# Causal attention on one Trainium2 core: scores from 64 contraction rows per head, two heads on the two halves of TensorE's rows

## The chip, the cores and the metric

The kernel runs on one core of one Trainium2 chip. The metric is the device time of one execution in microseconds (us), given as the median of several runs. The engines are PE (TensorE: matrix products and transposes), ACT (ScalarE), DVE (VectorE), POOL (GpSimd) and SP, whose queue issues the DMAs. PEld in the profile is PE's loading of weights. The memories on the core are SBUF (128 partitions), and PSUM, into which PE writes, in banks of 128 x 512 float32.

## The reference, cut to what matters

One block of a Perceiver-like model on 256 tokens of width 512: a cross-attention with sigmoid weights over 25,088 context rows, a causal self-attention with 16 heads, a compressed key/value path and rotary parts, and a mixture of eight experts of which each token takes one. The change lies in the second line.

```python
x = x + xattn(layernorm(x), ctx, ctx, Wq, bq, Wk, bk, Wv, bv)      # over 25,088 context rows
x = x + attn(layernorm(x), W_kv_down, W_k_up, W_v_up, W_q, W_q_rope, W_k_rope, W_o)
x = x + ffn(layernorm(x), gate_w, wg, wu, wd)

def attn(x, ...):                                     # D_C = 128, D_R = 32, NH = 16, HD = 32
    c_kv = x @ W_kv_down
    k_rope = rotary(c_kv @ W_k_rope)                  # one for all heads
    k = (c_kv @ W_k_up).reshape(B, T, NH, HD)
    v = (c_kv @ W_v_up).reshape(B, T, NH, HD)
    q = (x @ W_q).reshape(B, T, NH, HD)
    q_rope = rotary(x @ W_q_rope)                     # one for all heads
    scores = einsum('bqhd,bkhd->bhqk', q, k) + einsum('bqr,bkr->bqk', q_rope, k_rope)[:, None]
    scores = where(causal, -inf, scores / sqrt(HD + D_R))
    w = softmax(scores)
    return einsum('bhqk,bkhd->bqhd', w, v).reshape(B, T, 512) @ W_o
```

A head's scores are a product over 64 numbers: 32 of its own query and key, and the 32 rotary ones that all heads share.

## The kernel before, in words

**Main loop.** The context is taken in 49 chunks of 512 rows. Products of the first stage are made of three float32r matmuls on high and low parts (`mm3`, L98 to L100). The loop ends in a stretch written as named steps, and only this stretch is changed.

**Order table.** All after the loop is cut into steps, functions such as `Sp`, `Sv` or `PTc`. The string `ORDER` lists their calls, `name:arguments`, and this list is the program order; `in_order` pins every engine to it. A last argument `a` or `v` puts a copy on ACT or DVE. The engines run their parts of the list side by side and wait for each other by data. The 256 tokens are two halves, called chains 0 and 1 (argument `tt`).

**Steps of the attention**, for chain `tt`:
- `Vp`, `N1v`, `N1g`, `N1w`, `Xp`, `Xc`: end of the cross-attention, layer norm, transposed activations `xT`.
- `CKp`/`CKc`: `c_kv`. `Kp`/`Kc`: keys of all heads, product and copy into the score operand. `VSp`/`VSc`: values. `Qp`/`Qc`: queries of the 16 heads as four groups `g` of four heads.
- `KRp`, `KRv`, `KRc` and `QRp`, `QRv`, `QRc`: rotary keys and queries: product, rotation on DVE with the table `trig`, copies into the score operands.
- `Sp` (scores and mask), `Sv` (row maximum, DVE), `Sa` (exponentials with sums, ACT), `PTp`/`PTc` (transposed weights), `PVp` (weights times values). Chain 0 has 128 keys and four units `u` of four heads; chain 1 has 256 keys and eight units of two heads.
- `R1v`, `R2p`, `R2c`, `ATv`, `ATa`, `ATw`, `WOp`: normalisation and output product. `N2v` and the rest: layer norm, routing (`LG`, `RK`, `RW`, `RP`), gathering tokens by expert (`GA`), expert products (`GU`, `DN`) and putting back (`SC`, `OU`). `WOs`, `RWs`, `RDs` issue DMAs on SP: output weights, and the weights of experts chosen at run time (`mg`, `mh`, `md`).

**Score operands before.** A query tile `qs` of 128 partitions holds, for two heads at a time, their 64 own rows and the rotary rows, with zeros elsewhere (POOL memset, L359). The key tiles `kbd` hold in a column block per head its own 32 rows, the rotary rows in the other half of the partitions, and zeros (memset, L340). One float32 matmul over 128 rows gives the scores of two heads:

```python
for h in range(h0, h0 + n, 2):
    mm(p3[:, h - h0:h - h0 + 2, :], lhsT=qs[:, tt, h // 2, g, :], rhs=kbd[g // 2][:, g % 2, h:h + 2, :nk], ...)
```

`bank()` takes one of six PSUM banks shared by all steps; `pr` (exponentials) and `pt` (their transposes) each have two buffers.

Of the kernel before, what the change touches and what calls it, by code (L numbers as in the profile page):

```python
# [37 lines left out]
EXa ZSv ZSp O1:0:a AV:0 ZRv O2p:0 AV:1 O2a:0 AV:2 O2v:0 AV:3 Vp:0:0 Vp:0:1 Vp:0:2 Vp:0:3 AV:4 N1v:0 AV:5 AV:6  # L38
AV:7 N1g:0 N1w:0 O1:1:a Xp:0 O2p:1 Xc:0:a O2a:1 CKp:0 O2v:1 Qp:0:0 CKc:0:v Kp:0:0 Kp:0:1 Kc:0:0:3:a Kc:0:0:1:v
Vp:1:0 Kc:0:1:1:a Kc:0:1:3:v Vp:1:1 Vp:1:2 Vp:1:3 VSp:0 WOs N1v:1 Qp:0:1 VSc:0:a Qp:0:2 N1g:1 Qp:0:3 N1w:1 Xp:1  # L40
Qc:0:0:a Qc:0:1:v KRp:0 QRp:0 Xc:1:a KRv:0 QRp:1 KRc:0:1:0:v KRc:0:0:0:a QRv:0 Kc:0:1:2:a CKp:1 Kc:0:0:2:a
KRc:0:0:1:v QRc:0:0:v QRc:0:1:a Qp:1:0 Kc:0:0:0:a QRv:1 CKc:1:a KRc:0:1:1:v Kp:1:0 QRc:1:1:v QRc:1:0:a Kp:1:1
Kc:0:1:0:a Sp:0:1 Sp:0:3 Kc:1:0:3:a Sv:0:1 Sa:0:1 Sp:0:2 Sv:0:3 Kc:1:1:3:v Qp:1:1 Sa:0:3 Kc:1:1:1:v Sv:0:2
Qp:1:2 PTp:0:3 PTp:0:1 Sa:0:2 PTc:0:3:v Qp:1:3 PTc:0:1:v PVp:0:3 Qc:1:0:a Qc:1:1:v PVp:0:1 KRp:1 PTp:0:2 KRv:1
Sp:0:0 PTc:0:2:a KRc:1:1:0:v KRc:1:1:1:v Kc:1:1:2:a VSp:1 KRc:1:0:1:v Kc:1:1:0:a Kc:1:0:1:a Sv:0:0 Sp:1:4
Kc:1:0:0:a VSc:1:a KRc:1:0:0:v Kc:1:0:2:v Sa:0:0 Sp:1:6 Sv:1:4 Sp:1:2 Sv:1:6 Sa:1:4 R1v:0 PTp:0:0 Sp:1:1 Sv:1:2
Sa:1:6 PTc:0:0:v R2p:0 Sv:1:1 PTp:1:6 R2c:0:a Sp:1:7 Sa:1:2 Sp:1:5 Sv:1:7 PTp:1:2 Sv:1:5 Sp:1:3 Sa:1:7 PVp:0:2
Sv:1:3 PVp:0:0 PTc:1:6:a PTp:1:7 ATv:0 PTc:1:2:a PTp:1:4 Sa:1:5 PVp:1:6 PVp:1:2 PTc:1:4:v Sp:1:0 ATa:0 PTc:1:7:v
Sa:1:1 PTp:1:5 ATw:0 PVp:1:4 Sa:1:3 PVp:1:7 Sv:1:0 WOp:0:0 PTc:1:5:v WOp:0:1 PTp:1:3 PTp:1:1 PTc:1:3:a WOp:0:2
Sa:1:0 WOp:0:3 PVp:1:5 R1v:1 PVp:1:3 PTc:1:1:a PTp:1:0 N2v:0 R2p:1 PTc:1:0:a PVp:1:1 R2c:1:a PVp:1:0 ATv:1 N2g:0  # L50
ATa:1 N2w:0 Ya:0 ATw:1 Yp:0 Yv:0 Yc:0:a WOp:1:0 WOp:1:1 WOp:1:2 WOp:1:3 LGp:0 N2v:1 LGv:0 N2g:1 RKp:0 N2w:1
RKv:0 Yp:1 Ya:1 RWv:0 Yc:1:a RPv:0 RWs:0 LGp:1 Yv:1 PMp:0 GAp:0:0 LGv:1 PMc:0:a GAp:0:1 GAc:0:0:v GAp:0:2
GAc:0:1:a RKp:1 GAp:0:3 GAc:0:2:v GUp:0:0:0 RKv:1 GAc:0:3:a GUp:0:0:1 RWv:1 GUp:0:0:2 RPv:1 RWs:1 GUp:0:0:3
GUp:0:1:0 GEa:0:0 GUp:0:1:1 GEv:0:0 GUp:0:1:2 GUp:0:1:3 GAp:1:2 GEa:0:1 RDs:0 GAp:1:3 GEv:0:1 GAc:1:2:a GAp:1:0
GAc:1:3:a GAp:1:1 GAc:1:0:v ITp:0:1 ITp:0:0 PMp:1 GAc:1:1:a ITc:0:1:v ITc:0:0:v GUp:0:2:0 PMc:1:a GUp:0:2:1
GUp:0:2:2 GUp:0:2:3 DNp:0:0 GEa:0:2 GEv:0:2 GUp:1:1:0 DNa:0:0 RDs:1 GUp:1:1:1 GUp:1:1:2 DNv:0:0 GUp:1:1:3
GUp:1:2:0 GEa:1:1 GUp:1:2:1 GEv:1:1 GUp:1:2:2 GUp:1:2:3 GUp:1:0:0 GEa:1:2 GUp:1:0:1 GEv:1:2 GUp:1:0:2 GUp:1:0:3
DNp:0:1 GEa:1:0 GEv:1:0 ITp:0:2 SCp:0:0:0 DNa:0:1 SCp:0:0:1 ITc:0:2:v ITp:1:0 ITp:1:1 ITp:1:2 DNv:0:1 SCp:0:1:0
ITc:1:0:a ITc:1:2:a DNp:0:2 ITc:1:1:a DNp:1:0 DNa:0:2 DNp:1:1 DNv:0:2 DNa:1:0 DNp:1:2 DNv:1:0 DNa:1:1 SCp:0:1:1
DNa:1:2 DNv:1:1 SCp:0:2:0 SCp:0:2:1 SCp:1:0:0 DNv:1:2 SCp:1:0:1 SCp:1:1:0 SCp:1:1:1 OUv:0 SCp:1:2:0 SCp:1:2:1  # L60
OUs:0 OUv:1 OUs:1
# [17 lines left out]
def body(ctx, tc, a, out, nch=NCH):  # L79
# [25 lines left out]
    def bank(name):  # L105
        return psum.tile([P, D], F32, tag="b", name=name, bufs=6)
# [4 lines left out]
    def toks(t):  # L111
        return slice(t * P, (t + 1) * P)
# [225 lines left out]
    kbd = [sb.tile([P, 2, 4, T], F32, tag="rT", name=f"kbd{i}", bufs=2) for i in range(2)]  # L338
    for i in range(2):
        nc.gpsimd.memset(kbd[i], 0.0)  # L340
# [14 lines left out]
    trig = sb.tile([64, T], F32, tag="qp0", name="trig")  # L355
    nc.sync.dma_start(trig, a["trig"])
    vs = [sb.tile([P, D], F32, tag=f"kp{i}", name=f"vs{i}", bufs=2) for i in range(2)]
    qs = sb.tile([P, 2, 2, KD, P], F32, tag="N0", name="qs", bufs=2)
    nc.gpsimd.memset(qs, 0.0)  # L359
# [95 lines left out]
    @step  # L455
    def N1v(tt):
        tt2(x1[tt], ps_["v", tt], x_sb[tt], ALU.add)
        mo[tt] = var(x1[tt], f"b{tt}")
# [22 lines left out]
    def rotated(n, dst, ps, tt):  # L481
        c = sb.tile([32, P], F32, tag="rc", name=f"rc{n}{tt}")
        s = sb.tile([32, P], F32, tag="rsn", name=f"rsn{n}{tt}")
        tt2(c, ps[0:32], trig[0:32, toks(tt)], ALU.mult)
        tt2(s, ps[32:64], trig[32:64, toks(tt)], ALU.mult)
        tt2(dst, c, s, ALU.add)
# [13 lines left out]
    @step  # L500
    def QRp(tt):
        ps_["qr", tt] = bank(f"qr_ps{tt}")[0:64, 0:P]
        prod(ps_["qr", tt], tt, lambda j: pw["wqr"][:, 64 * j:64 * (j + 1)])

    @step
    def QRv(tt):
        qr[tt] = sb.tile([32, P], F32, name=f"qr{tt}")
        rotated("q", qr[tt], ps_["qr", tt], tt)

    @step  # L510
    def QRc(tt, i, eng):
        r = 64 - 64 * i
        scaled(eng, qs[r:r + 32, tt, i], qr[tt][:, None, :].broadcast_to([32, KD, P]), 0.125)
# [11 lines left out]
    @step  # L525
    def KRc(tt, h, i, eng):
        r = 64 - 64 * i
        cp[eng](kbd[h][r:r + 32, :, 2 - r // 32:4 - r // 32, toks(tt)], kr[tt][:, None, None, :].broadcast_to([32, 2, 2, P]))

    @step  # L530
    def Kp(tt, h):
        ps = ps_["k", tt, h] = bank(f"k_ps{tt}{h}")[:, :2 * P].rearrange("p (g t) -> p g t", g=2)
        for g in range(2):
            mm(ps[:, g, :], lhsT=pw["wku"][:, toks(2 * h + g)], rhs=ckv[tt], start=True, stop=True)

    @step
    def Kc(tt, h, j, eng):
        r = slice(32 * j, 32 * j + 32)
        cp[eng](kbd[h][r, :, j, toks(tt)], ps_["k", tt, h][r])
# [16 lines left out]
    @step  # L556
    def Qc(tt, i, eng):
        r = slice(64 * i, 64 * i + 64)
        scaled(eng, qs[r, tt, i], ps_["q", tt][r], 0.125)
# [3 lines left out]
    pr, pt, sc, mx = {}, {}, {}, {}  # L563

    def heads(tt, u):
        return (u, 0, 4) if tt == 0 else (u // 2, 2 * (u % 2), 2)

    @step
    def Sp(tt, u):
        g, h0, n = heads(tt, u)  # L570
        nk = P * (tt + 1)
        p3 = sc[tt, u] = bank(f"s{tt}_{u}").rearrange("p (h k) -> p h k", h=n)
        if tt == 0:
            mm(p3, lhsT=identb, rhs=mask[:, None, :].broadcast_to([P, n, P]), start=True, stop=False)
        for h in range(h0, h0 + n, 2):
            mm(p3[:, h - h0:h - h0 + 2, :], lhsT=qs[:, tt, h // 2, g, :], rhs=kbd[g // 2][:, g % 2, h:h + 2, :nk],  # L576
               start=tt == 1, stop=tt == 0 and h == 2)
        if tt == 1:
            mm(p3[:, :, P:], lhsT=identb, rhs=mask[:, None, :].broadcast_to([P, n, P]), start=False, stop=True)

    @step
    def Sv(tt, u):
        mx[tt, u] = sm.tile([P, 4], F32, tag="mx", name=f"mx{tt}_{u}", bufs=4)
        nc.vector.tensor_reduce(mx[tt, u][:, :heads(tt, u)[2]], sc[tt, u], AX.X, ALU.max, negate=True)

    @step
    def Sa(tt, u):
        g, h0, n = heads(tt, u)
        pr[tt, u] = sb.tile([P, D], F32, tag="wr", name=f"pr{tt}_{u}", bufs=2).rearrange("p (h k) -> p h k", h=n)
        for i in range(n):  # L590
            h = 4 * g + h0 + i
            nc.scalar.activation(pr[tt, u][:, i, :], sc[tt, u][:, i, :], AF.Exp, bias=mx[tt, u][:, i:i + 1],
                                 accum_out=sums[:, tt, h:h + 1])

    @step
    def PTp(tt, u):
        ps = ps_["pt", tt, u] = bank(f"pt{tt}_{u}")
        for i in range(heads(tt, u)[2]):
            for kt in range(tt + 1):
                nc.tensor.transpose(ps[:, toks(i * (tt + 1) + kt)], pr[tt, u][:, i, toks(kt)], ident)  # L600

    @step
    def PTc(tt, u, eng):
        pt[tt, u] = sb.tile([P, D], F32, tag="z", name=f"pt{tt}_{u}", bufs=2)
        cp[eng](pt[tt, u], ps_["pt", tt, u])

    @step
    def PVp(tt, u):
        g, h0, n = heads(tt, u)
        if pv[tt] is None:  # L610
            pv[tt] = psum.tile([P, KD, P], F32, tag=f"acc{tt}", name=f"pv{tt}")
        for kt in range(tt + 1):
            for i in range(n):
                r = slice(32 * (h0 + i), 32 * (h0 + i + 1))
                mm(pv[tt][r, g, :], lhsT=vs[kt][:, g * P + r.start:g * P + r.stop],  # L615
                   rhs=pt[tt, u][:, toks(i * (tt + 1) + kt)], start=kt == 0, stop=kt == tt)
# [41 lines left out]
    @step  # L658
    def N2v(tt):
        x2[tt] = sb.tile([P, D], F32, tag=f"x{tt}", name=f"x2{tt}")  # L660
        tt2(x2[tt], ps_["wo", tt], x1[tt], ALU.add)
        mo[tt] = var(x2[tt], f"c{tt}")
# [279 lines left out]
```

## Time and profile before

| what | value |
|---|---|
| median of 3 runs | 581.35 us (580.42 to 581.46) |
| the profiled execution | 580.47 us, span 578.5 us |
| PE, DVE, ACT busy | 560.4, 447.3, 388.0 us |
| scores, lines L576 (PE), busy in 490 to 545 us | 8.1 us in 16 passes of 512 columns, 4.1 us in 16 of 256 columns |
| masks, L574 and L579 | 1.5 and 2.2 us |
| first score matmul, first output product of chain 1 (`WOp:1`) | 507.5 us, 540.2 us |

The span runs from the first to the last instruction of one profiled execution; the time of the execution is 2.0 us longer. Times of instructions are given from the start of the span. Matmuls overlap, so their busy time is more than the pace at which they follow each other; the chain of waits gives the pace. A float32 matmul appears as two instructions, called passes below.

### The profile page before, as it was taken

How to read it: one execution, taken by the hardware profiler on the slowest of the kernel's cores; microseconds unless marked ns; L12 is line 12 of the kernel's file. 1: busy time of each engine (PE TensorE's matmuls, PEld its weight loads, DVE VectorE, ACT ScalarE, POOL GpSimd, SP SyncE). 2: the span in 40 equal slices, each digit the busy share in tenths (PEclk: the TensorE clock that was granted, in tenths of full speed). 3: DMA queues.
4: the chain of work that ended last, by engine and by line, in shares of the span. 5: the costliest groups of instructions: out<-in, count | busy, mean ns of one | idle time of the engine just before them, and what ended most of it. 6: DMA issues, size and time to landing. Idle time of an engine off the chain costs nothing.

```text
span 578.5 us, 7915 instructions
## 1 busy us (share of the span) xinstructions
PE 560.4 (97%) x3044; PEld 465.3 (80%) x3044; DVE 447.3 (77%) x513; ACT 388.0 (67%) x497; POOL 22.5 (4%) x36
## 2 busy tenths in 40 slices
PE   4999999999999999999999999999999999999697
PEld 3888888888888888888888888888888887876563
DVE  5899888878787878787878787878787865575754
ACT  5877777777777777777777777777777763376332
POOL 5200000000000000000000000000000023000000
PEclk9999999999999999999999999999999999999889
DMA  8897878876575656565657575756465554300081
GB/s 285 347 368 277 288 278 304 304 257 254 183 251 187 255 180 253 187 247 188 248 190 252 181 254 184 256 181 255 180 257 181 213 193 175 146 2 1 5 306 56
DMA packets 22725, 124.49 MB, mean 215 GB/s; under 512 B 3040, under 2 KB 3232, under 8 KB 9376
## 3 DMA queue, kind: packets, MB, share of 16 engines
q1 hardware_dynamic: 22688, 123.99, 59.4%
q8 instruction: 24, 0.39, 0.3%
q14 instruction: 13, 0.11, 0.1%
HBM read 121.36 MB, written 2.62 MB: 214 GB/s over the span
## 4 chain that ended last, share of the span: by engine, by line
PE 94%; DVE 3%; issue 1%; ACT 1%; DMA 1%; POOL 0%; SPq 0%; DVEq 0%; ACTq 0%; POOLq 0%
PE acc L98 15%; PE acc L99 15%; PE acc L100 15%; PE kp_ps L99 8%; PE kp_ps L98 8%; PE kp_ps L100 8%; PE sc L100 4%; PE sc L99 4%; PE sc L98 4%; PE s L576 2%; PE gu L813 2%; PE q_ps L479 1%; PE pt L600 1%; PE dn L842 1%; PE pv L615 1%
## 5 line engine op out<-in xcount | busy, mean ns | idle before, releaser
L95 DVE TENSOR_TENSOR N<-rN,N 128x2048 fp32r<-128x2048 f32 (+1 forms) x53 | 111.8, 2114 | 57.7 <-ACT N L94 57.6
L98 PE MATMUL acc<-N,z 128*128 128x512 f32 x392 | 153.9, 393 | 0.0
L99 PE MATMUL acc<-N,z 128*128 128x512 f32 x392 | 153.7, 392 | 0.0
L100 PE MATMUL acc<-N,z 128*128 128x512 f32 x392 | 152.5, 389 | 0.0
L95 DVE TENSOR_TENSOR T<-rT,T 128x2048 fp32r<-128x2048 f32 (+1 forms) x49 | 110.3, 2253 | 17.2 <-ACT T L94 17.2
L220 ACT ACTIVATE z<-sc 128x512 f32<-128x512 f32 x98 | 58.7, 599 | 78.8 <-PE sc L100 78.6
L94 ACT CAST N<-rN 128x2048 fp32r<-128x2048 f32 (+1 forms) x55 | 94.4, 1725 | 6.1
L94 ACT CAST T<-rT 128x2048 fp32r<-128x2048 f32 (+1 forms) x55 | 94.1, 1717 | 0.1
L100 PEld LDWEIGHTS acc<-N,z 128*128 128x128 f32 x392 | 73.6, 188 | 16.1
L98 PEld LDWEIGHTS acc<-N,z 128*128 128x128 f32 x392 | 74.0, 189 | 12.3
L99 PEld LDWEIGHTS acc<-N,z 128*128 128x128 f32 x392 | 74.0, 189 | 11.6
L98 PE MATMUL kp_ps<-T,wk 128*128 128x512 f32 x196 | 76.9, 392 | 0.0
L100 PE MATMUL kp_ps<-T,wk 128*128 128x512 f32 x196 | 76.7, 391 | 0.0
L99 PE MATMUL kp_ps<-T,wk 128*128 128x512 f32 x192 | 74.7, 389 | 0.0
L222 DVE TENSOR_TENSOR zacc<-zacc,z 128x512 f32<-128x512 f32 x98 | 67.5, 688 | 7.0 <-ACT z L220 1.5
L95 DVE TENSOR_TENSOR z<-z,z 128x512 fp32r<-128x512 f32 x98 | 67.5, 689 | 0.0
L94 ACT CAST z<-z 128x512 fp32r<-128x512 f32 x98 | 61.0, 623 | 3.1
L211 ACT ACTIVATE kp<-kp_ps,bk 128x512 fp32r<-128x512 f32 x49 | 33.9, 691 | 39.9 <-PE kp_ps L100 39.9
L100 PE MATMUL sc<-qp,kp 128*128 128x256 f32 x196 | 55.8, 285 | 0.1
L99 PE MATMUL sc<-qp,kp 128*128 128x256 f32 x196 | 55.4, 283 | 0.0
L98 PE MATMUL sc<-qp,kp 128*128 128x256 f32 x196 | 54.9, 280 | 0.0
L98 PEld LDWEIGHTS kp_ps<-T,wk 128*128 128x128 f32 x196 | 37.1, 189 | 7.8
(209 smaller groups left out, 561.8 us busy)
## 6 DMA issues: line engine op xcount, KB each, us to landing
rN<-in_ctxN SPq DMA_DIRECT2D x49, 1024.0 KB, 4.8
rT<-in_ctxT SPq DMA_DIRECT2D x47, 1024.0 KB, 4.9
gu<-in_gu SPq DMA_DIRECT2D x4, 1024.0 KB, 7.2
sp_wo<-w_wo SPq DMA_DIRECT2D x8, 256.0 KB, 4.0
wo<-sp_wo SPq DMA_DIRECT2D x2, 1024.0 KB, 6.0
mg<-in_gu SPq DMA_DIRECT2D x4, 512.0 KB, 4.0
md<-in_dn SPq DMA_DIRECT2D x6, 256.0 KB, 7.2
rT<-in_ctxT SPq DMA_DIRECT2D x4, 256.0 KB, 6.1
```

The lines of the kernel that those rows point to most:

```text
L94: copy(hi, src)
L95: eng.tensor_tensor(lo, src, f(hi), ALU.subtract)
L98: mm(ps, lhsT=ahi, rhs=bhi, start=first, stop=False)
L99: mm(ps, lhsT=ahi, rhs=blo, start=False, stop=False)
L100: mm(ps, lhsT=alo, rhs=bhi, start=False, stop=last)
L211: nc.scalar.activation(kp[c][0], ps, AF.Identity, bias=bk)
L220: nc.scalar.activation(z, ps, AF.Sigmoid, scale=1.0 / math.sqrt(128.0))
L222: tt2(zacc, zacc, z, ALU.add)
L479: mm(ps, lhsT=w(j), rhs=xT[tt][:, j, :], start=j == 0, stop=j == KD - 1)
L576: mm(p3[:, h - h0:h - h0 + 2, :], lhsT=qs[:, tt, h // 2, g, :], rhs=kbd[g // 2][:, g % 2, h:h + 2, :nk], start=tt == 1, stop=tt == 0 and h ...
L600: nc.tensor.transpose(ps[:, toks(i * (tt + 1) + kt)], pr[tt, u][:, i, toks(kt)], ident)
L813: mm(gps[tt, g][r, :], lhsT=yg[tt][:, j, at], rhs=w[:, 2 * j * P:2 * (j + 1) * P], start=j == 0, stop=j == KD - 1)
```

## The change

Each head gets 64 rows of its own: 32 of the head and 32 rotary. Of a group's four heads, 0 and 1 lie in partitions 0 to 63, heads 2 and 3 in 64 to 127; in the second head of each half the two parts are swapped (`sides`). No zeros are needed, and the memsets are gone. One key tile `ks` replaces the two `kbd`. `Sp` takes two units at a time, one on each half of the rows, into two banks, and issues their matmuls by turns. `PVp` takes two units too. `QRp` makes the rotary queries of both chains in one bank, chain 1 in partitions 64 to 127, for which `trig` is loaded twice. `Kc` and `Qc` become copies of 32 partitions by 512; `QRc` and `KRc` likewise, four for a chain. Chain 1 has four buffers for `pr` and `pt`, and `mx` eight. `N1v` and `N2v` lose their variance to steps `N1s` and `N2s`. The order table is new as a whole; of it only the part around the attention is shown.

```diff
@@ ORDER, the attention @@
-... N1w:0 O1:1:a Xp:0 O2p:1 Xc:0:a O2a:1 CKp:0 O2v:1 Qp:0:0 CKc:0:v Kp:0:0 Kp:0:1 ... Vp:1:0 ... Xp:1 ...
-... QRv:1 CKc:1:a KRc:0:1:1:v Kp:1:0 QRc:1:1:v QRc:1:0:a Kp:1:1 Kc:0:1:0:a Sp:0:1 Sp:0:3 ... Sp:0:2 ...
-... VSp:1 KRc:1:0:1:v Kc:1:1:0:a Kc:1:0:1:a Sv:0:0 Sp:1:4 Kc:1:0:0:a VSc:1:a KRc:1:0:0:v ...
+... N1w:0 O1:1:a Xp:0 O2p:1 Xc:0:a O2a:1 CKp:0 O2v:1 Qp:0:0 CKc:0:a Vp:1:0 Vp:1:1 Vp:1:2 Vp:1:3 Kp:0
+WOs N1v:1 Qp:0:1 N1s:1 Kc:0:0:a Kc:0:3:a Qp:0:2 N1g:1 Kc:0:1:a Qp:0:3 N1w:1 Kc:0:2:a Xp:1 Qc:0:1:a VSp:0 Xc:1:v
+Qc:0:2:a Qc:0:0:a KRp:0 VSc:0:v QRp Qc:0:3:a KRv:0 KRc:0:0:v KRc:0:2:a KRc:0:1:v Qp:1:0 KRc:0:3:v QRv:0 Qp:1:1
+QRc:0:1:v QRc:0:0:a QRv:1 Qp:1:2 QRc:0:2:a QRc:0:3:v QRc:1:0:v QRc:1:1:a Qp:1:3 QRc:1:2:v QRc:1:3:a Sp:0:1
+Qc:1:2:a Qc:1:1:a Qc:1:3:a CKp:1 Sv:0:2 Qc:1:0:a Sv:0:3 Sa:0:2 Sp:0:0 CKc:1:v KRp:1 Sa:0:3 Sv:0:1 Kp:1 KRv:1
+VSp:1 Kc:1:1:a Sv:0:0 Kc:1:3:a PTp:0:3 KRc:1:2:v KRc:1:0:v PTp:0:2 Kc:1:2:a KRc:1:1:v KRc:1:3:v Kc:1:0:a
+PTc:0:2:v Sa:0:1 PTc:0:3:v Sp:1:1 VSc:1:v Sa:0:0 PVp:0:1 Sv:1:3 PTp:0:1 Sv:1:2 Sa:1:3 Sp:1:0 ...
...
+... Yp:1 Ya:1 RPv:0 Yc:1:a LGp:1 RWv:0 GAp:0:0 LGv:1 GAp:0:3 RWs:0 ... RPv:1 ... RWv:1 ... RWs:1 ...
...
-    kbd = [sb.tile([P, 2, 4, T], F32, tag="rT", name=f"kbd{i}", bufs=2) for i in range(2)]
-    for i in range(2):
-        nc.gpsimd.memset(kbd[i], 0.0)
+    ks = sb.tile([P, 2, KD, T], F32, tag="rT", name="ks", bufs=2)
...
-    nc.gpsimd.memset(qs, 0.0)
...
+    def QRp():
+        ps_["qr"] = bank("qr_ps")[:, 0:P]
+        for j in range(KD):
+            for t in range(2):
+                mm(ps_["qr"][64 * t:64 * t + 64], lhsT=pw["wqr"][:, 64 * j:64 * (j + 1)], rhs=xT[t][:, j, :],
+                   start=j == 0, stop=j == KD - 1)
...
+    sides = [(e, 64 * i + 32 * e, 64 * i + 32 - 32 * e) for e in range(2) for i in range(2)]
...
+    def KRc(tt, i, eng):
+        e, _, r = sides[i]
+        cp[eng](ks[r:r + 32, e, :, toks(tt)], kr[tt][:, None, :].broadcast_to([32, KD, P]))
...
+    def Kc(tt, i, eng):
+        e, r, _ = sides[i]
+        cp[eng](ks[r:r + 32, e, :, toks(tt)], ps_["k", tt][r:r + 32])
...
+    def heads(tt, u):
+        k, i = divmod(u, 2)
+        return [4 * g + 2 * i + e for g in ((2 * k, 2 * k + 1) if tt == 0 else (k,)) for e in range(2)]
+
+    def Sp(tt, k):
+        nk = P * (tt + 1)
+        hs = [heads(tt, 2 * k + i) for i in range(2)]
+        n = len(hs[0])
+        p3 = [bank(f"s{tt}_{2 * k + i}").rearrange("p (h k) -> p h k", h=n) for i in range(2)]
...
+        for j in range(n):
+            for i in range(2):
+                g, h = divmod(hs[i][j], 4)
+                r = slice(64 * i, 64 * i + 64)
+                mm(p3[i][:, j, :], lhsT=qs[r, tt, h % 2, g, :], rhs=ks[r, h % 2, g, :nk],
+                   start=tt == 1 and j == 0, stop=tt == 0 and j == n - 1)
...
+    def PVp(tt, k):
+        units = (2 * k, 2 * k + 1)
+        n = len(heads(tt, 2 * k))
+        for kt in range(tt + 1):
+            for j in range(0, n, 2):
+                for u in units:
+                    for i in (j, j + 1):
+                        g, h = divmod(heads(tt, u)[i], 4)
+                        r = slice(32 * h, 32 * h + 32)
+                        mm(pv[tt][r, g, :], lhsT=vs[kt][:, g * P + r.start:g * P + r.stop],
+                           rhs=pt[tt, u][:, toks(i * (tt + 1) + kt)], start=kt == 0, stop=kt == tt)
```

In the new table a unit pair `k` stands behind `Sp` and `PVp` (`Sp:1:1` makes units 2 and 3), a unit behind `Sv`, `Sa`, `PTp` and `PTc`.

## The prediction

> **What bounds the kernel now.** I read the page first, then the chain of waits from 485 us on, then the windows of that stretch, then the timelines of PE and of its weight loads.
>
> ```profile
> PE 560.4 (97%) x3044; PEld 465.3 (80%) x3044; DVE 447.3 (77%) x513; ACT 388.0 (67%) x497; POOL 22.5 (4%) x36
> ```
>
> PE is busy for 97% of the span. The diff touches nothing before the order table, whose PE work begins near 485 us, so only the last 90 us count. Windows over them:
>
> ```profile
> core 0: us, PE busy (x) PEld busy (x) DVE busy (x) ACT busy (x) POOL busy (x), PEclk, DMA share, GB/s
> ...
> 507.00:517.50 10.50, 10.50 (x81) 8.87 (x80) 7.04 (x16) 7.68 (x32) 0.00 (x0) 1.00 0.01 2
> 517.50:526.00 8.50, 8.50 (x38) 4.43 (x36) 6.92 (x13) 6.46 (x27) 0.00 (x0) 1.00 0.00 0
> 526.00:538.00 12.00, 11.95 (x125) 8.65 (x123) 6.78 (x13) 8.03 (x25) 0.55 (x1) 1.00 0.01 1
> ...
> 543.00:546.00 3.00, 0.93 (x9) 0.76 (x8) 2.79 (x10) 0.00 (x0) 0.55 (x1) 0.98 0.00 0
> 546.00:548.00 2.00, 1.10 (x5) 0.73 (x5) 1.70 (x12) 1.20 (x2) 0.00 (x0) 0.50 0.00 0
> ```
>
> From 507 to 538 us, the causal attention, PE never stops, while ACT has 31.0 - 22.2 = 8.8 us free. PE work taken out there shortens the kernel until ACT or DVE is late. The last two rows matter for a rival: after PE was busy for only 0.93 of 3 us, the granted clock fell to 0.50.
>
> The chain of waits prices PE's pieces at their pitch:
>
> ```profile
> 508.77 0.86 PE s L576 x4
> ...
> 514.27 0.57 PE pv L615 x16
> 514.84 0.36 PE kr_ps L518 x2
> 515.21 0.59 PE pt L600 x4
> ...
> 517.73 0.86 PE s L576 x2
> 518.59 0.11 PE s L579
> ...
> 520.64 0.44 PE pt L600 x4
> ...
> 527.98 1.00 PE pv L615 x16
> ```
>
> Two score matmuls of 256 columns are 4 passes (0.215 each), one of 512 is 2 passes (0.43 each). So a pass costs 0.107 us per 128 columns. Sixteen passes of `pv`, each 32 columns wide in the array, would be 1.71 us in series: 0.57 with four column tiles at work (0.036 a pass), 1.00 with two (0.0625). Tiles therefore do run side by side here.
>
> PE and its weight loads:
>
> ```profile
> 514.77 0.19 PEld L518 LDWEIGHTS kr_ps<-ckv,wkr 128*64 128x64 f32 x2 [0.20 <-issue]
> ```
>
> ```profile
> 542.78 0.95 PE L699 MATMUL lg_ps<-gate,yT 128*128 128x8 f32 x8
> ```
>
> The first shows that loads stop for 0.20 us where the tile shape changes. The second has eight passes of only 8 columns in 0.95 us, so a load of 128 weight columns needs about 0.107 us by itself.
>
> **The change part by part.**
>
> *Scores of chain 1 (`Sp:1`).* Before: 8 x (0.86 + 0.11) = 7.8 us. After: 32 passes of 256 columns, in pairs on the two row halves, and the same masks. No row tile is in this trace. Bounds: in series 32 x 0.215 = 6.9 us, nothing gained; perfectly paired 3.4. The nearest row is `pv` on two tiles, 0.0625 per 128 columns, so 0.125 x 32 = 4.0 us. Gain 2.85. Serial weight loads (32 x 0.107 = 3.4) would fit under that.
>
> *Scores of chain 0 (`Sp:0`).* Before: 4 x 0.86 = 3.4 us beside the masks. After: 32 passes of 128 columns; by `pv` 2.0 us, gain 1.4. Here weight loads decide. By the `lg_ps` row, 32 loads of 0.107 make 3.4 us if they queue, gain 0. The Trainium skill (TensorE: Matmul & The Clock Gate, "LDWEIGHTS") speaks against the change: a load takes time by its columns and is not shorter with fewer rows. The row agrees at 128 rows. But TensorEngine Tiling (Array Packing), "Key Properties", lets different tiles load in parallel, which no row here shows. By the one 0, by the other 1.4; lying between, I take 0.7 and keep both ends.
>
> *Shape changes.* `pv` to `kr_ps` to `pt` above costs 0.36 instead of 0.21 for two passes and 0.59 instead of 0.44 for four transposes, 0.15 each. Each of the six `Sp` now sits between full-array work: 12 changes x 0.15 = 1.8 us more. The same tiling page, "Key Properties", says that changing the mode drains the engine; this trace says how much, and left out, the forecast would be 1.8 us lower. Bounds: 12 x 0.10 to 12 x 0.20.
>
> *`PVp` by unit pairs.* The six pieces of `pv` in the chain sum to 4.7 us; after, all 96 passes run on four column tiles, 6 x 0.57 = 3.4, and the pieces stand in five groups instead of six, 0.3 less in changes. Gain 1.55.
>
> *`QRp` once for both chains.* 16 passes in series take 1.84 us (502.02 to 503.86); on two column halves at 0.0625, 1.0. Gain 0.85. It now waits for `Xc:1`.
>
> PE sum: 2.85 + 0.7 + 1.55 + 0.85 - 1.8 = 4.15 us less; with the ends of the terms, between 2.8 and 6.0.
>
> *Copies.* `Kc` goes from 16 of 32x256 (11 on ACT, 0.36 each, 5 on DVE, 0.42) to 8 of 32x512, all ACT; `Qc` from 4 of 64x512 to 8 of 32x512, all ACT; `QRc` from 4 to 8 (ACT 0.63, DVE 0.41); `KRc` stays at 8; `VSc` goes from ACT to DVE. Back-to-back ACT copies out of PSUM start 0.48 to 0.50 apart (536.68 and 537.16). ACT: Kc 3.9 against 4.2, Qc 3.9 against 1.0, QRc 2.5 against 1.3, VSc 0 against 1.0, so about 2.8 us more; DVE 1.4 less. Of ACT's 8.8 us about 2 are left once the stretch is 4 us shorter. Not free, so I walked the new order with these durations, 0.2 us from PE's pitch end to a reader.
>
> *The walk.* `Vp:1` goes ahead of `Kp:0` and ends at 496.95 (before 497.7); `Xp:1` 500.5; `QRp` 502.2 to 503.2; `Qp:1` until 506.9. The first scores need the last `QRc:0`, DVE, 507.25, so they begin at 507.5, like before (507.7). ACT has then without a break 4 `QRc`, 4 `Qc:1`, `Sa:0:2`, `Sa:0:3` (1.38 each) and 4 `Kc:1`, from 505.6 to 514.9. `Sp:1:1`, the first of chain 1, takes two PSUM banks. Just ahead of it all six are alive (`s` of two units, `k`, `vs` and two `pt`), so it also waits for `PTc:0:2`, which DVE reaches only after `KRv:1`, `Sv:0:0` and four `KRc:1`: 515.8. It starts at 515.85 (before, `Sp:1:4` at 517.6), and PE has been idle since `PTp:0:2` at 514.3, 1.5 us. From there PE leads again: `WOp:0` near 528, the last `PVp` until 534.2, `ATv:1` and `ATw:1` after it. `WOp:1` starts at 536.2 against 540.2: 4.0 us. With queued weight loads in `Sp:0`, `Kp:1` ends at 514.2, `PTc:0:2` at 517.5, and `WOp:1` comes 1.7 us later: 2.3 us. Middle 3.15; I take off 0.35 for hops that the walk holds for nothing: 2.8 us.
>
> *Edits that I cost at nothing.* Gone on POOL are two memsets of `kbd` (1.82 each, 475.8 and 477.5) and that of `qs` (1.81, 485.0): POOL idles 1.40 us before its next duty at 489.6, covered by PE. Where a buffer's release now falls first on a copy, it has lain free for 10 us. `trig` is two DMAs on SP instead of one (issue 0.56, landing 7.1 from 477.9), needed at 502.7. `WOs` moves by 0.7 us with the end of `Vp:1`; landing 6.0, needed at 527; behind it on SP only `RWs` waits, at 548. `N1s` and `N2s` are the same DVE instructions, let apart. Four buffers for `pr` and `pt` and eight for `mx` only remove waits; PSUM stays at six banks; elsewhere than at `Sp:1:1` the walk finds at most five alive.
>
> *After attention.* The work is the same and the number of tile blocks in the expert part too. `RPv` now precedes `RWv`, so `RWs:0` on SP (548.32 before) comes 1.6 us later against its stage, `RWs:1` (555.13) about 1.0, and behind them the six `md` DMAs (556.80, 2.99 of issue, 7.2 landing). `mg` and `mh` land 4.0 to 5.4 after issue; those of chain 1 were needed at 563.1 and there by 561.7, so 0.4 us of slack stay. If that cover is gone `GUp:1:2` waits as long. `GAc` all on ACT (0.5 each) keeps pace with `GAp`. I take 0; bounds -2 (the half clock from 546 to 552 may fall shorter) to +1.
>
> Sum: 580.47 us of the profiled execution (span 578.5, 2.0 around it) minus 2.8 is 577.7. That execution lies 0.9 under the median 581.35, at the low end of 580.42 to 581.46; I give 577.8.
>
> **The rivals.**
>
> *A. The row halves don't overlap (0.12).* Then the change doesn't do what it says. For: no row tile in the trace. Against: column tiles overlap. PE: 1.55 + 0.85 - 1.8 = 0.6 less, eaten by the 1.5 of new idle time: 580.5 + 0.9 = 581.4, no change.
>
> *B. ACT becomes the bound (0.13).* For: 2.8 us more on it, and a chain of fourteen operations ahead of `Sp:1:1`. Against: from 505.6 to 534 its work is 22.6 us, 80%. If its waits grow all along, 2 us of the gain go: 579.8.
>
> *C. The clock halves in the attention (0.12), the slower side.* If the wait ahead of `Sp:1:1` leaves PE idle for 2 us or more in some 3 us, as at 543 to 546, the clock falls to 0.50 for about 6 us, as it did there (eight `lg_ps` passes then took 1.88 instead of 0.95). That is 3 us more PE time, and up to 2 of longer idling: 577.8 + 5 = 582.8. The walk's idle time of 1.5 us is three quarters of that point. The Trainium skill (TensorE: Matmul & The Clock Gate, "What's actually happening") makes low activity in one window of about 3.4 us the cause; by it a pause of 1.5 us, with busy PE on both sides of it, costs nothing, and the rows at 543 and 546 don't contradict it.
>
> **How the numbers follow.** The forecast, 575.5 to 579.3, has 0.63, A 0.12, B 0.13, C 0.12. The range reaches down to perfect pairing and parallel loads (6.0 us on PE less half a us of new idle time: 575.0), and up over A: 575.0 to 581.8. About 0.2% (1.2 us) is what a measurement of this kernel can tell from no change. Faster by more: the forecast and most of B, 0.74; within: A and a little of B, 0.12; slower: C and the tail of A, 0.14.
>
> **What would show it.** Right: two score matmuls on different halves starting less than 0.1 us apart; `Sp:1` near 1.0 us plus masks for four heads; `pv` 0.57 for every 16 passes; `qr_ps` near 1.0; `WOp:1` near 536.5. LDWEIGHTS of the two halves 0.107 apart in `Sp:0` would confirm the lower end. Wrong: PE idle before `Sp:1:1` far over 1.5 us with ACT as releaser (B), a granted clock under 1 between 507 and 535 (C), score passes end to end (A), or PE waiting for `mg` near 560.

## The result, and the profile after

The changed kernel takes 575.93 us (median of 4 runs, 575.04 to 576.26), the kernel before 580.89 us in runs beside it (580.42 to 581.46). The ratio is 0.9912, 95% interval 0.9895 to 0.9929: 5.0 us faster, where 3.5 us had been forecast. The profiled execution took 576.25 us with a span of 574.3; against the profiled one of before (580.47) that is 4.2 us, because that one lay low in its runs and this one high.

The windows over the attention, from the profile after (columns as in the prediction):

```profile
500.00:507.00 7.00, 7.00 (x63) 5.96 (x63) 5.57 (x16) 4.58 (x8) 0.00 (x0) 1.00 0.52 219
507.00:514.20 7.20, 7.06 (x62) 5.07 (x61) 5.71 (x15) 7.00 (x25) 0.00 (x0) 1.00 0.00 0
514.20:522.00 7.80, 6.53 (x75) 4.79 (x75) 7.22 (x14) 7.78 (x33) 0.00 (x0) 1.00 0.00 1
522.00:533.00 11.00, 11.00 (x136) 8.41 (x126) 8.28 (x15) 7.77 (x26) 0.00 (x0) 1.00 0.01 1
```

PE still works nearly all the time, but in two rows the sixth column, ACT, is nearly full (7.00 of 7.20, 7.78 of 7.80). In the second of them PE has one hole. The timeline of PE shows it, at the first scores of chain 1:

```profile
507.32 1.20 PE L592 MATMUL s<-ks,qs 64*128 64x128 f32 x16
...
515.95 1.13 PE L592 MATMUL s<-ks,qs 64*128 64x256 f32 x8 [1.27 <-ACT ks L545]
```

Scores begin at 507.32 (predicted 507.5), `Sp:1:1` at 515.95 (predicted 515.85), after 1.27 us of idle PE (predicted 1.5). The releaser is ACT's copy of keys, `Kc:1`. The chain of waits gives the pace of what follows:

```profile
515.95 1.13 PE s L592 x8
517.09 0.32 PE s L596 x2
517.41 0.57 PE pv L638 x16
...
522.28 1.06 PE s L592 x8
523.34 0.33 PE s L596 x2
...
532.24 1.05 PE pv L638 x32
```

Four heads of chain 1 now take 1.06 us and 0.33 for two masks; before they took 2 x (0.86 + 0.11) = 1.94. `pv` runs at 0.53 to 0.57 for 16 passes throughout. The first output product of chain 1, `WOp:1`, starts at 535.44 in this chain, against 540.19: 4.75 us earlier. From the end of that product to the end of the span it is 36.1 us, before 35.5: about 0.6 us are given back in the routing stage, where the clock is at half for 6.8 us in both kernels (545.9 to 552.7 before, 543.0 to 549.85 after). Two kernels further down, in which the clock is held, show that this is the cause. Here PE has work during all of it:

```profile
543.00:545.00 2.00, 2.00 (x10) 2.00 (x10) 1.26 (x6) 0.00 (x0) 0.00 (x0) 0.50 0.00 0
```

### The profile page after: what moved, and what is told of

The parts are those of the page before. It is cut to its first block, busy times and chain, and to the rows that moved or that the text cites. A ratio compares the mean times of both kernels' runs of the same rounds, so it can differ in the third digit from the quotient of the medians.

```text
span 574.3 us, 7962 instructions
## 1 busy us (share of the span) xinstructions
PE 555.5 (97%) x3076; PEld 462.1 (80%) x3076; DVE 446.8 (78%) x512; ACT 390.7 (68%) x498; POOL 17.3 (3%) x33
```

## Experiments

Theory 1 is that the gain comes from score matmuls running on both halves of the rows at once. Its rival is that paired `PVp`, the shared `QRp` and the new order bring it. Beside it stood the terms of the prediction's sum: the price of a shape change, the ACT queue ahead of `Sp:1:1`, and the half clock. Unless said otherwise each kernel is the changed one with one edit, and times are medians. A second clock, used to compare single executions, is the time since the first pass of `kr_ps` or `qr_ps`, since these passes come up to 0.7 us earlier or later from one execution to the next: by PE's timeline `WOp:1` starts 33.3 us after them in the changed kernel (535.20 and 501.88).

### All score matmuls on one half

```diff
-                r = slice(64 * i, 64 * i + 64)
+                r = slice(0, 64)
```

> Every score matmul reads its queries and keys from partitions 0 to 63, so that two neighbours never stand on different halves; heads 2 and 3 of each group get the scores of heads 0 and 1 (that part of the computation is changed). Theory 1 (the gain is the overlap of the two halves): each Sp takes 1.7 us for its score passes, 4.5 us more on PE and 3 to 4.5 us more in all, ratio 0.997 to 1.000. Rival (most of the 5 us comes from the paired PVp, the shared QRp and the new order): at most 2 us more, ratio under 0.9945. Sp waits here only for the copies of the lower halves, so up to 0.6 us of the idle time ahead of Sp:1:1 may go, against theory 1.

Measured: 586.33 us (ratio 1.0073, interval 1.0045 to 1.0102), slower than the kernel before and 10 us slower than the changed one, more than twice what theory 1 wanted. PE's timeline shows why:

```profile
517.36 2.33 PE L592 MATMUL s<-ks,qs 64*128 64x256 f32 x8 [0.69 <-DVE ks L534]
...
521.88 3.78 PE L592 MATMUL s<-ks,qs 64*128 64x256 f32 x8
```

The second piece takes 3.78 us. The windows give the cause:

```profile
522.00:527.00 5.00, 5.00 (x15) 3.73 (x16) 2.24 (x5) 0.71 (x4) 0.00 (x0) 0.50 0.00 0
```

The granted clock, third column from the end, fell to 0.50, from about 520.15 to 530.4 us, in the midst of the attention. This is rival C, which the changed kernel had escaped. (In the routing stage, too, the clock is at half for longer here, 10.2 us from 550.9 on.) One of the six runs, with a mean clock of 0.991 instead of 0.982, took 581.05.

### One half, with PE kept busy ahead of Sp:1:1

```diff
-                r = slice(64 * i, 64 * i + 64)
+                r = slice(0, 64)
...
-PTc:0:2:v Sa:0:1 PTc:0:3:v Sp:1:1
+PTc:0:2:v Sa:0:1 PTc:0:3:v FIp:7 Sp:1:1
...
+    def FIp(n):
+        ps = bank(f"fill{n}")
+        for _ in range(n):
+            nc.tensor.transpose(ps[:, 0:P], ident, ident)
```

> As e2_one_half (heads 2 and 3 of each group get the scores of heads 0 and 1), with seven transposes of the identity, 0.77 us, in the pause of PE ahead of Sp:1:1; nothing reads them. In e2_one_half the clock fell to 0.50 from about 520.4 to 530.5 us after a pause of only 0.7 us. Theory (the pause sets it off): the clock stays 1.00 in the attention, 580.5 to 582 us, which is then the price of the lost overlap alone, 5 us. Rival (passes on half of the rows in series count as little activity, whatever the pause): the clock falls as before, about 586.5 us.

Measured: 581.58 us (21 runs, ratio 1.0007, interval 1.0000 to 1.0013). The clock stays at 1.00 in the attention, and both kinds of score piece have the duration of passes in series:

```profile
507.63 2.05 PE L598 MATMUL s<-ks,qs 64*128 64x128 f32 x16
...
517.06 0.98 PE L582 MATMUL fill<-ident 128*128 128x128 f32 x7 [0.70 <-ACT ks L545]
518.10 1.99 PE L598 MATMUL s<-ks,qs 64*128 64x256 f32 x8
```

```profile
522.00:527.00 5.00, 5.00 (x45) 4.06 (x45) 4.07 (x8) 3.54 (x15) 0.00 (x0) 1.00 0.02 3
```

The transposes were meant to fill the pause and did not. They too had to wait, by the trace for ACT's last copy of keys (probably for the PSUM bank that it reads), so that the pause stays at 0.70 us, and then they stand between it and `Sp:1:1`. They have a price: on the second clock the mask of `Sp:1:1` starts at 17.83 us, in the experiment above at 17.13, with the clock still at 1.00 there. So the overlap of the halves is worth 581.58 - 575.93 = 5.65 us less these 0.7, about 4.9 us. Without the overlap and without the transposes the change would, by this estimate, be worth nothing: 580.9, the time of the kernel before; rival A of the prediction gave 581.4. The rival to theory 1 falls.

For the clock, neither expectation is shown. The pause is the same in both kernels and so are the passes in series, but the clock fell in five of six runs above and in none of the 21 here. What differs is the transposes between the two, on the full array, and a second gap: above, the third pass of `Sp:1:1` starts at 518.14, though the second, begun at 517.68, needs only 0.215 us (it waits for a PSUM bank, as in the next experiment). Which of these decides is open.

### The halves one after the other

```diff
-        for j in range(n):
-            for i in range(2):
+        for i in range(2):
+            for j in range(n):
```

> Sp issues all matmuls of the lower half of the rows, then all of the upper half, instead of by turns; nothing else changes. Theory 1 (matmuls start in program order, and only neighbours on different halves overlap): 16 passes take about 1.7 us instead of 0.98 in Sp:0 and 8 passes about 1.7 instead of 0.92 in Sp:1, 6 x 0.75 = 4.5 us more on PE; about 1 us of it falls into the idle time ahead of Sp:1:1 or is given back at the boundary of the halves, so the kernel is 3 to 4.5 us slower than the changed one: 579 to 580.5 us, ratio to the kernel before 0.997 to 1.000. Rival (each half works off its own queue, whatever the order): within 0.5 us of the changed kernel, ratio 0.991 to 0.992.

Measured: 577.06 us (ratio 0.9930, interval 0.9917 to 0.9943), only 1.1 us slower than the changed kernel. Both expectations miss. The timeline of PE has three answers in it:

```profile
507.84 1.71 PE L592 MATMUL s<-ks,qs 64*128 64x128 f32 x16
...
516.60 1.90 PE L592 MATMUL s<-ks,qs 64*128 64x256 f32 x8 [0.70 <-DVE ks L534]
...
519.91 1.14 PE L592 MATMUL s<-ks,qs 64*128 64x256 f32 x8
```

With eight passes in a row on one half, more than half of the overlap is gone (1.71; by turns 1.16 to 1.20, in series 2.05): the upper half starts 0.56 us after the lower. With four in a row it is whole in three of the four pieces (1.14, as by turns), where both halves start together (519.91 and 519.92 in the second). In the first piece, `Sp:1:1`, it is nearly gone (1.90). There the fifth pass, the first of the upper half, starts at 517.37, just after DVE has finished `PTc:0:2` (at 517.31), whose PSUM bank `Sp:1:1` needs:

```profile
516.62 0.69 DVE L624 COPY pt<-pt 128x512 f32<-128x512 f32 x1
...
517.37 0.70 PE L592 MATMUL s<-ks,qs 64*128 64x256 f32 x2
```

So this piece waits for a bank, and says nothing of the order of issue. Strict turns are not what makes the overlap: it reaches over four passes, and not over eight; what sets this reach was not tested. What `Sp:0` loses falls into the pause, which is 0.70 us instead of 1.27, so that little more than the 0.77 us of `Sp:1:1` arrives: on the second clock `WOp:1` comes 0.9 us later.

### PVp by unit, and units apart

```diff
-        for kt in range(tt + 1):
-            for j in range(0, n, 2):
-                for u in units:
+        for u in units:
+            for kt in range(tt + 1):
+                for j in range(0, n, 2):
```

> PVp takes its two units one after the other instead of mixing them; order table and all else as in the changed kernel. Prediction's term: pv 0.57 for 16 passes becomes 1.0 in the four pieces of chain 1 (4 x 0.43 = 1.7 us) and stays about 0.57 in chain 0 or grows to 1.0 (2 x 0.43); from 526 us on PE leads, so the kernel gets 1.3 to 2.2 us slower: ratio 0.9934 to 0.995. Rival (column tiles further apart in the queue overlap too, as PVp:1:4 next to PVp:1:7 did in the kernel before with 0.59): under 0.7 us, ratio under 0.9924.

Measured: 575.86 us (ratio 0.9913, interval 0.9900 to 0.9925), the changed kernel's time. `pv` keeps its pace:

```profile
524.15 0.66 PE L638 MATMUL pv<-ptb,vs 128*32 128x128 f32 x16
```

The mixing is worth nothing. What the new `PVp` does bring is that two units on different column tiles stand next to each other in PE's queue. Pulling them apart tests that (`PVu` is `PVp` for one unit):

```diff
-R2c:0:v PTp:1:0 ATv:0 PTp:1:1 PTc:1:0:a Sv:1:6 PVp:1:1 PTc:1:1:a Sv:1:7 Sp:1:2 ATa:0 Sa:1:7 ATw:0 PVp:1:0 Sv:1:4
-Sa:1:6 WOp:0:0 Sv:1:5 ...
+R2c:0:v PVu:1:2 PTp:1:0 ATv:0 PTp:1:1 PTc:1:0:a Sv:1:6 PVu:1:3 PTc:1:1:a Sv:1:7 Sp:1:2 ATa:0 PVu:1:0 Sa:1:7 ATw:0 WOp:0:0 PVu:1:1 Sv:1:4
+Sa:1:6 Sv:1:5 ...
```

> The two units of PVp:1:1 and of PVp:1:0 stand apart, with transposes or an output product between them; the rest as in the changed kernel. e3_pv_by_unit showed that mixing the units within PVp is worth nothing. Theory (two units that stand next to each other in PE's queue overlap, two that stand apart can't): each unit alone takes about 0.45 us for 8 passes instead of 0.285, and each of the two extra visits brings two changes of 0.15: 2 x (0.33 + 0.3) = 1.3 us slower than the changed kernel, 577.0 to 577.5. Rival (pv was never a limit there, PE waits for ACT): under 0.5 us.

Measured: 577.68 us (ratio 0.9952, interval 0.9939 to 0.9966), 1.75 slower and a little above what the theory gave, and `WOp:1` 1.4 us later on the second clock. Each unit alone, of half as many passes, holds PE as long as two together:

```profile
522.91 0.63 PE L642 MATMUL pv<-ptb,vs 128*32 128x128 f32 x8
```

### QRp in series

```diff
-        for j in range(KD):
-            for t in range(2):
+        for t in range(2):
+            for j in range(KD):
```

> QRp makes all four products of chain 0 and then the four of chain 1, in the same bank, instead of by turns. Theory 1: its 16 passes take 1.8 us instead of 1.06, first scores 0.75 us later, and as ACT's chain to Sp:1:1 (which starts with QRv:0, whose product is ready earlier) sets the next wait, only a part of it arrives: 0.2 to 0.8 us slower than the changed kernel, ratio 0.9916 to 0.9926. Rival (the rotary part is hidden): within 0.2 us, ratio 0.9912.

Measured: 576.27 us (ratio 0.9923, interval 0.9906 to 0.9939). The interval holds both expectations. On the second clock the first scores come 0.5 us later, `Sp:1:1` at the same time, since the ACT queue ahead of it starts with chain 0's rotary queries, which are ready no later, and `WOp:1` 0.3 us later. These 0.3 us arise in `Sp:1:1`, which takes 1.41 us instead of 1.13: its second pass starts only at 516.28, when DVE has finished `PTc:0:2` (516.23); in the changed kernel the first two start together. `kr_ps` and `qr_ps` fill 1.73 us of PE (501.92 to 503.65) where it was 1.24 by turns and 2.11 before: a good half of what `QRp` saves is due to the turns.

### More shape changes

```diff
+            if j == n // 2:
+                mm(p3[0][:, 0, 0:8], lhsT=identb, rhs=none, start=False, stop=False)
```

> In the middle of each Sp one full-array matmul of 8 columns adds zeros to the scores: 12 more changes of the tile shape, and 6 x 0.1 us at most for the matmul and its load. Theory (a change costs 0.15 us whichever tile): 12 x 0.15 = 1.8 us more on PE plus 0.1 to 0.6 for the matmuls, some of it in the idle time ahead of Sp:1:1: 1.2 to 2.4 us slower than the changed kernel, 577.1 to 578.3. Rival (changes to row tiles are free, since a full matmul and a half one only wait for the same rows): 0 to 0.6 us slower.

Measured: 578.12 us (ratio 0.9949, interval 0.9936 to 0.9962), 2.2 us slower.

```profile
506.96 0.75 PE L596 MATMUL s<-ks,qs 64*128 64x128 f32 x8
507.65 0.18 PE L592 MATMUL s<-none,identb 128*128 128x8 bf16 x1
507.76 0.71 PE L596 MATMUL s<-ks,qs 64*128 64x128 f32 x8
```

On the second clock `WOp:1` comes 1.7 us later; in the routing stage of this execution the clock was at half for 10.2 us, not 6.8, so the kernel's 2.2 us may hold a part that is not of the edit. A chain-1 piece from its first pass to its mask grows from 1.07 to 1.38 us (518.92 to 520.30): 0.31 for two changes and one matmul of 8 columns with its weight load. Changes to row tiles are not free; 0.15 each is the upper end, since the small matmul is in it.

### ACT relieved

```diff
-... KRc:0:0:v KRc:0:2:a KRc:0:1:v Qp:1:0 KRc:0:3:v QRv:0 ... VSp:1 Kc:1:1:a Sv:0:0 Kc:1:3:a ... PTc:0:2:v Sa:0:1
+... KRc:0:0:v KRc:0:2:a KRc:0:1:a Qp:1:0 KRc:0:3:a QRv:0 ... VSp:1 Kc:1:1:a Kc:1:3:a ... PTc:0:2:v Sv:0:0 Sa:0:1
```

> Order table only: KRc:0:1 and KRc:0:3 go from DVE to ACT, which idles from 504.1 to 505.7 us, so that DVE reaches QRv:0 0.85 us earlier; Sv:0:0 moves on DVE from ahead of the KRc:1 to behind PTc:0:2. Theory (the fourteen ACT operations from QRc to Kc:1 set the start of Sp:1:1, and the bank of PTc:0:2 is next): ACT's chain and with it Sp:1:1 starts 0.6 to 0.85 us earlier than 515.95, idle PE ahead of it 0.5 instead of 1.3 us, kernel 0.4 to 0.85 us faster than the changed one. Rival (PE leads in the stretch and what is won is idled away ahead of the next exponential): within 0.2 us.

Measured: 576.27 us, with an interval of the ratio (0.9907 to 0.9937) that leaves 0.3 us either way open. On the second clock `Sp:1:1` and `WOp:1` come 0.41 us earlier, less than the theory gave for `Sp:1:1` and the low end of what it gave for the kernel; the pause is still 1.27 us instead of the 0.5 expected, because the transposes ahead of it wait for the same ACT queue. That this did not reach the median goes with the clock: three executions with a mean clock of 0.994 took 575.1 to 575.5 us, three with 0.991 took 577.05 to 577.44. How long the half clock lasts weighs more here than the edit.

### PE kept busy in the routing stage

```diff
-LGp:0 N2v:1 N2s:1 LGv:0 N2g:1 N2w:1 RKp:0 RKv:0 Yp:1 Ya:1 ...
+LGp:0 FIp:14 N2v:1 N2s:1 LGv:0 N2g:1 N2w:1 RKp:0 FIp:3 RKv:0 Yp:1 FIp:5 Ya:1 ...
```

> 22 transposes of the identity into a spare bank stand where PE waits after the attention: 14 (1.5 us) behind LGp:0, 3 behind RKp:0, 5 behind Yp:1; nothing reads them. Theory (the half clock from 543 to 550.5 us is the answer to PE's being busy for only about 2 of the 5 us from 538 to 543): the granted clock stays 1.00, PE's 7 us at half clock shrink by up to 3.5, of which copies on ACT and the landing of the expert weights hold back some: 1.5 to 3.3 us faster than the changed kernel, 572.7 to 574.5 us. Rival (the clock falls for another reason, or at a fixed place): clock still 0.50, 0 to 0.5 us slower.

Measured: 573.43 us (573.12 to 573.84, ratio 0.9871, interval 0.9857 to 0.9885), 2.5 us faster than the changed kernel.

```profile
538.00:543.00 5.00, 4.44 (x40) 3.87 (x38) 4.34 (x19) 1.21 (x2) 0.55 (x1) 1.00 0.00 0
543.00:545.00 2.00, 2.00 (x17) 1.94 (x16) 1.83 (x9) 0.69 (x2) 0.00 (x0) 1.00 0.00 0
```

PE is busy for 4.44 of the 5 us ahead, and the clock stays at 1.00 where it was 0.50. In the changed kernel it is busy for about 2 of them:

```profile
538.00:541.00 3.00, 1.08 (x11) 0.96 (x10) 2.55 (x9) 0.00 (x0) 0.55 (x1) 1.00 0.00 0
541.00:543.00 2.00, 0.94 (x8) 0.64 (x7) 1.76 (x11) 1.20 (x2) 0.00 (x0) 1.00 0.00 0
```

No kernel of the study is clearly faster. The same transposes in the kernel before:

> The kernel before with the same 22 transposes behind LGp:0, RKp:0 and Yp:1 as in e5_fill. Theory (the half clock in the routing stage has nothing to do with the change): 2.0 to 3.0 us faster than the kernel before, 578 to 579 us, so the change is worth 4.5 to 5.5 us with or without it. Rival (the change itself moved the half clock): under 1.5 or over 3.5 us.

Measured: 578.13 us (ratio 0.9954, interval 0.9941 to 0.9967), 2.8 us faster than the kernel before. With PE filled on both sides the change is worth 578.13 - 573.43 = 4.7 us, so its gain does not come from a shifted clock. The two traces also settle the 0.6 us given back in the routing stage: from the first pass of `lg_ps`, behind `WOp:1`, to the end of the span it is 33.5 us in both (538.01 to 571.5 and 543.01 to 576.5), where without the filling it is 36.3 in the changed kernel and 35.7 in the one before. With the clock held nothing is given back. The two edits together:

> The edits of e5_fill and e6_act_relief together. If both theories hold the gains add: 2 to 4 us faster than the changed kernel, 572 to 574 us, ratio to the kernel before 0.985 to 0.988. If the clock falls elsewhere, as e6 alone.

Measured: 573.59 us (ratio 0.9879, interval 0.9864 to 0.9893). The relief of ACT adds nothing that can be seen in the time.

## Why the prediction was right, step by step

**The bound.** PE set the end in the attention, and taking its work out shortened the kernel. Right: 4.75 us at `WOp:1`. The range held, and the size was short, 3.5 us against 5.0.

**`Sp:1`.** Forecast 4.0 us of passes, 0.9 of masks and eight changes of 0.15, 6.1 in all; measured, changes included, 4.3 us of passes and 1.3 of masks, 5.6. The passes are paired almost perfectly, a little better than `pv` on two tiles.

**`Sp:0`.** Here lay the term that was most mis-sized. I put its gain at 0.7 us, between weight loads that queue (0) and loads that run side by side (1.4). PE's weight loads after, and below them those of the kernel that uses one half with the transposes:

```profile
507.32 1.01 PEld L592 LDWEIGHTS s<-ks,qs 64*128 64x128 f32 x16 [0.42 <-ACT qs L376]
...
507.63 1.86 PEld L598 LDWEIGHTS s<-ks,qs 64*128 64x128 f32 x16 [0.42 <-ACT qs L376]
```

Sixteen loads, of 0.19 us each in the profile, are done in 1.01 us, so they begin 0.055 apart; on one half it is 1.86 us and 0.11, and a load of 128 columns needed 0.107 by the `lg_ps` row. The sign that I had named for queued loads, 0.107 apart, did not appear. Loads to different halves overlap, as the Trainium skill has it (TensorEngine Tiling (Array Packing), "Key Properties"). Its other rule, that a load costs by its columns and not by its rows (TensorE: Matmul & The Clock Gate, "LDWEIGHTS"), agrees with the 0.11 of one half, but the passes alone would give that pace too. Sixteen passes and two masks of `Sp:0:1` fill 506.80 to 508.45, 1.65 us with both changes, where two pieces of before took 2.15. Over both pieces that is 1.0 us of gain after changes; the prediction had 0.1. These pieces lie ahead of the pause, so their gain does not simply add up at the end: by the walk, queued loads would have moved `WOp:1` by 1.7 us.

**Shape changes.** 0.10 into the row tiles (506.80 and two masks of 0.21 end at 507.22, scores start at 507.32). Out of them it is about 0.14 here (the last two passes start at 508.20, the next product at 508.45, and a pair takes 0.107) and 0.10 in `Sp:1`. The price of 0.15 was near, and rather high.

**`PVp`.** The size was right (4.7 to 3.3 us in the chain), the reason half wrong: not the mixing, but two units standing side by side in the queue.

**`QRp`.** `kr_ps` and `qr_ps` together went from 2.11 us (501.75 to 503.86) to 1.24 (501.88 to 503.12): 0.87, forecast 0.85.

**The walk.** `Sp:1:1` began at 515.95 against 515.85, after a pause as forecast. This agreement is in part luck. In the walk ACT's last copy of keys was done at 514.9, and the PSUM bank of `PTc:0:2`, at 515.8, decided. DVE did finish that at 515.75, but ACT's last copy ended only at 515.9 and decided:

```profile
513.56 2.34 ACT L545 COPY ks<-k_ps 32x512 f32<-32x512 f32 x4
...
515.06 0.69 DVE L624 COPY pt<-pt 128x512 f32<-128x512 f32 x1
```

The step that failed is the price of ACT's copies: four of 32 x 512 out of PSUM begin 0.58 to 0.60 us apart, where 0.48 to 0.50 had been taken over from copies of 128 x 512. Both waits are real. With ACT relieved the bank is free at 514.59, ACT's last copy ends at 514.97 and the scores start at 515.03; with the halves one after the other, and with `QRp` in series, the bank comes later than ACT and holds up the upper half.

`WOp:1` came 0.8 us earlier than the 536.2 of the walk, and `WOp:0` had already come 0.9 earlier than its 528; between `Sp:1:1` and there the quicker passes of `Sp:1` explain 0.5, the rest was not traced. The rest of the way from the 2.8 us forecast for `WOp:1` to the 4.75 measured is what the forecast had taken off: 0.85 for the chance of queued loads (4.0 to 3.15) and 0.35 for hops.

**After the attention.** Forecast 0, measured 0.6 us worse in the profiled execution, by the place of the half clock; with the clock held the stretch is the same in both kernels. The loads of expert weights were not late: PE goes on without a pause through `gu` and `dn`.

**Rivals.** A is where the change goes if its overlap is taken away (580.9 by the estimate above, 581.4 given), though the pause that A's sum puts at 1.5 us was 0.7 there. B was partly there, as 1.27 us of pause with ACT as releaser; after it PE did not wait until 533. C came true in an experiment, in a kernel that had lost the overlap too: against 580.9 its 586.3 is 5.4 us more (4.8 of them up to `WOp:1` on the second clock), where the prediction gave the half clock 5. The size agrees although the clock stayed down for 10.2 us instead of the 6 of the estimate. Its point of decision was wrong. I had put it at 2 us of pause; there it fell after 0.69 us and a second, shorter gap, with passes in series on half of the rows, while 1.27 us with both halves at work never did it in any trace here. That a short pause between busy stretches costs nothing, as the prediction had it, held for 1.27 us and failed for 0.69 with a second gap behind it.

## What to carry to other kernels

When small contractions leave half of PE's rows empty, put two of them on the two halves (here each had its own PSUM bank; a shared one was not tried), and place them close to each other in PE's order; the same holds for column tiles, where it is the neighbourhood in the queue that counts. Charge every stay in another tile shape with two changes (here 0.20 to 0.25 us together) and group the work by shape. Price a copy by one of its own shape. And look at the granted clock behind every stage where PE waits: some transposes that nobody reads were worth half as much as the whole change.

## What the runs showed of the hardware that I had not expected

The half clock comes in steps: 6.8 us in the routing stage of both kernels, 10.2 us there in the kernel with more shape changes, and 10.2 us both there and in the attention in the kernel with one half: two and three times 3.4 us. The Trainium skill gives a window of 3413 ns for the clock gate (TensorE: Matmul & The Clock Gate, "What's actually happening"), which these lengths agree with. That PE is busy by the profile does not protect it: in the kernel with one half PE was busy for 4.67 of 5 and 4.56 of 5 us around the fall. Seven transposes behind the same pause held the clock in the attention, by the times of all 21 runs (580.54 to 582.31), with no more busy time (4.36 and 4.88 of 5 us in the same windows). With the halves one after the other, a pause of the same length (0.70) and a first piece of 1.90 us left the clock at 1.00 in the attention of the traced run. Whether half-filled passes count for less activity or whether the pause fell at a bad place in a window is open; these runs fit either.
